# A graph-attention layer with a residual and layer norm: a bound on the scores from sums of squares, W in one transfer, and fewer stores

## The chip, the cores and the metric

The kernel runs on one core of a Trainium2 chip. A core has five engines that run side by side, each through its own list of instructions in order: TensorE (PE, matrix products), VectorE (DVE), ScalarE (ACT), GpSimd (POOL) and SyncE (SP, which here does nothing but issue transfers). Transfers between the large memory (HBM) and the core's own memory run on 16 DMA engines. Matrix products go to a small memory of their own, PSUM. The metric is the device time of one execution in microseconds; lower is better.

## What is computed

`x` is 4096 x 512, `adj` is 4096 x 4096 and stands for a matrix that is added to attention scores, `W` is 512 x 2048 (four heads of 512 columns), `a` is 4 x 1024.

```python
ht = (h @ W).reshape(N, N_HEADS, N_HIDDEN).transpose(1, 0, 2)
src = jnp.einsum('hnd,hd->hn', ht, a[:, :N_HIDDEN, 0])
dst = jnp.einsum('hnd,hd->hn', ht, a[:, N_HIDDEN:, 0])
e = jax.nn.leaky_relu(src[:, :, None] + dst[:, None, :], SLOPE) + adj_mat[None]
att = jax.nn.softmax(e, axis=-1)
h_prime = jnp.einsum('hij,hjd->hid', att, ht)
x = _layernorm(x + h_prime.mean(axis=0), axis=-1)
```

The entries of `adj` are either 0 or random numbers up to 1e9, which is far more than any score from `src` and `dst`. Where the largest entry of a row leads the second by more than the scores can make up, the softmax is exactly 1 at that place and 0 elsewhere. The row's result is then the layer norm of `x` of that row plus (the row of `x` that the largest entry points at) times (the mean of W over the heads).

## The kernel before

The kernel has a fast path, `leading_rows`, and a full one, `general`, which runs only if some row fails the test for a lead (line 66).

*Tiling.* The 4096 rows are 32 blocks of 128, one row a partition. A partition holds the rows 32p to 32p+31, so block `ib` takes the row 32p+ib of each partition, 16 KB of `adj`. The loop (line 432) has 32 steps; step `t` does several stages of different blocks: `segment_maxima` and `find_segment` of block t (VectorE reduces 4096 entries to maxima of segments of 16, 32 or 64, then finds the largest and its segment; GpSimd fetches that segment, `lead`, by an indirect transfer), `find_column` of block t-2 (the place within the segment; GpSimd gathers the row of `x` that it points at, `y`), `turn` and `products` of block t-3 (TensorE transposes `y`, adds `x` as the residual and multiplies by `w_sum`), `stats` of block t-4 and `finish` of two blocks from t-6 (ScalarE: mean, variance, scaling).

*Memory.* One large tile, `hold`, has 32 places of 512 numbers a partition. It first holds W in the places 16 to 31 (`w_at`), then `x` block by block, then the results. `adj` has six buffers (`AHEAD` + 1): the load of block t+6 waits until VectorE is done with block t.

*Order.* The order on each engine is the order in which the code is written (line 55). SP issues almost all transfers into one hardware queue: block 0 of `adj`, half of W, block 1, half of W, blocks 2 to 4, then `x` of blocks 0 to 3 (lines 132 to 143), later one block of `adj` in each step with a few loads of `x` between (line 427). ScalarE issues four loads of `a`, two rows each (line 135). In the built program eight completion semaphores serve the direct transfers of SP and ScalarE in turn, so that a transfer waits for the one that used its semaphore last. Stores are issued after the loop (lines 491 to 496 and 551 to 553).

*The bound.* `mean_of_heads` averages W into `w_sum` at steps 0 to 2. From step 0 to step 14, `turn_a` transposes `a`, and `turn_w` and `head_vector` form, head by head, the product of W's columns with the two halves of `a`: 16 times four transposes, one eviction by ScalarE and eight small products into `pv`. At step 16 `head_norms` takes from these vectors, `v`, the largest sum of norms over the heads, `vn`. After the loop `bound` multiplies `vn` by the largest norm of a row of `x` (`lead_by`), and `test`, `count` and `report` count the rows whose lead is too small. `v` is also handed to `general`.

*The tail.* After the loop come the last blocks: `BEHIND` = 24 and `LATE` = 28; x of blocks 28 to 31 is loaded at step 26, x of 24 to 27 at the last step. The results of blocks 0 to 23 are stored while TensorE and VectorE end blocks 28 to 31; those of 24 to 31 are stored last.

Of the kernel before, what the change touches and what calls it, by code (L numbers as in the profile page):

```python
# [9 lines left out]
F32 = mybir.dt.float32  # L10
# [10 lines left out]
P = 128  # L21
# [8 lines left out]
@with_exitstack  # L30
def gat_resnorm_kernel(
    ctx: ExitStack,
    tc: tile.TileContext,
    x: bass.AP,
    adj: bass.AP,
    W: bass.AP,
    a: bass.AP,
    out: bass.AP,
):

    nc = tc.nc
# [9 lines left out]
    v = keep.tile([P, KB, 2 * H], F32, name="v")  # L59
    n_bad = keep.tile([1, NB], I32, name="n_bad")  # L60
    any_bad = keep.tile([1, 1], I32, name="any_bad")

    leading_rows(tc, x, adj, W, a, out, ident, v, n_bad, any_bad)

    flag = nc.values_load(any_bad[0:1, 0:1], min_val=0, max_val=N)
    with tc.If(flag > 0, preferred_fallthrough_block=True, label="general"):
        general(tc, x, adj, W, out, ident, v, n_bad)


@with_exitstack  # L70
def leading_rows(ctx, tc, x, adj, W, a, out, ident, v, n_bad, any_bad):

# [34 lines left out]
    once.tile([P, 24], F32, name="pad")  # L107
# [5 lines left out]
    once.tile([P, 32], F32, name="pad_end")  # L113
    adj_t = {}

    def pieces(ib):
# [9 lines left out]
    def load_x(lo, n):  # L126
        nc.sync.dma_start(hold[:, ds(lo, n), :], x_rows[:, ds(lo, n), :])

    def load_w(kb, n):
        nc.sync.dma_start(hold[:, ds(w_at + kb * H, n * H), :], w_blocks[:, ds(kb * H, n * H), :])  # L130
# [12 lines left out]
    load_x(0, Q)  # L143

# [192 lines left out]
    def store(queue, lo, n):  # L337
        queue.dma_start(out_rows[:, ds(lo, n), :], hold[:, ds(lo, n), :])
# [7 lines left out]
    at_d = once.tile([P, KB, 2 * H], F32, name="at_d")  # L346
    vn = once.tile([P, 1], F32, name="vn")
    pv = psum.tile([P, KB, 2 * H], F32, name="pv", bufs=1)

    def turn_a():  # L350
        tp = psum.tile([P, KB, P], F32, name="tp", bufs=2)
        for k in range(KB):
            nc.tensor.transpose(tp[:, k, : 2 * H], a_rows[:, ts(k, P)], ident[: 2 * H, : 2 * H])
        nc.scalar.copy(at_d, tp[:, :, : 2 * H])

    def turn_w(kb, h):
        tp = psum.tile([P, KB, P], F32, name="tp", bufs=2)
        for k in range(KB):
# [5 lines left out]
    def head_vector(kb, h, wt):  # L364

        for k in range(KB):
            nc.tensor.matmul(  # L367
                pv[:, kb, h : 2 * H : H], wt[:, k, :], at_d[:, k, h : 2 * H : H],
                start=(k == 0), stop=(k == KB - 1),
            )  # L370

    def head_norms():
        nc.vector.tensor_copy(v, pv)
        vv = once.tile([P, KB, 2 * H], F32, name="vv")
        nc.vector.tensor_mul(vv, v, v)
        pn = psum.tile([P, KB, 2 * H], F32, name="px", bufs=1)
        nc.tensor.matmul(pn, ones, vv, start=True, stop=True)
        n2 = once.tile([P, 2 * H], F32, name="n2")
        nc.vector.tensor_reduce(n2, pn.rearrange("p k c -> p c k"), axis=AX.X, op=OP.add)
        nc.scalar.activation(n2, n2, AF.Sqrt)  # L380
# [47 lines left out]
    vectors = [(kb, h) for kb in range(KB) for h in range(H)]  # L428
    vectors_at = {t: 2 if t < 3 else 1 for t in range(1, 15)}
    COLUMN, PROJECT, STATS, FINISH = 2, 3, 4, 6  # L430

    for t in range(NB):
        if t == NB // 2:
            tc.mark_branch_hint_location("general", engines=HINTED)
        if t in x_at:
            load_x(*x_at[t])
        if t + AHEAD == NB - 1:
            load_x(LATE, Q)
        load_adj(t + AHEAD)
        middle = 1 if t == NB - 1 else 2  # L440
        segment_maxima(t, 0, middle)
        if t >= COLUMN:
            find_column(t - COLUMN)
        segment_maxima(t, middle, PIECES)
        pair = FINISH <= t < BEHIND + FINISH and t % 2 == 0
        if pair:
            rstd(slice(t - FINISH, t - FINISH + 2))
        if t == NB - 1:
            for ib in (BEHIND, BEHIND + 2):
                load_x(ib, 2)  # L450
        find_segment(t)
        if t < 2:
            mean_of_heads(t)
# [100 lines left out]


@with_exitstack
def general(ctx, tc, x, adj, W, out, ident, v, n_bad):

# [6 lines left out]
    nc = tc.nc  # L565
    N, D = x.shape
    KB, NB, NCH, Q = D // P, N // P, N // C, C // P
    H = v.shape[2] // 2
# [5 lines left out]
    w_sb = const.tile([P, KB, H * D], F32, name="w_sb")  # L574
    x_blocks = x.rearrange("(nb p) d -> p nb d", p=P)
    w_blocks = W.rearrange("(kb p) m -> p kb m", p=P)

    with ExitStack() as pre:
        sd_all = pre.enter_context(tc.tile_pool(name="all", bufs=1)).tile([2 * H, N], F32, name="sd_all")
# [3 lines left out]
            nc.gpsimd.dma_start(x_sb[:, ts(g, Q), :], x_blocks[:, ts(g, Q), :])  # L583
        for kb in range(KB):
            nc.gpsimd.dma_start(w_sb[:, kb, :], w_blocks[:, kb, :])
        for g in range(NCH):
            xT = two.tile([P, KB, C], F32, name="xT")
            for q in range(Q):
                ps = pps.tile([P, KB, P], F32, name="ps_x")
                for kb in range(KB):  # L590
                    nc.tensor.transpose(ps[:, kb, :], x_sb[:, g * Q + q, ds(kb, P, KB)], ident)
# [115 lines left out]
```

## Time and profile before

| what | value |
|---|---|
| median of 3 runs | 235.49 us (235.22 to 236.12) |
| the profiled execution | 234.9 us |
| its span, first to last instruction | 233.4 us |
| TensorE busy | 199.9 us (86%) |
| VectorE busy | 191.3 us (82%) |
| ScalarE busy | 111.8 us (48%) |
| GpSimd busy | 100.7 us (43%) |
| moved by DMA | 97.12 MB, mean 416 GB/s |
| of it through SP's queue | 88.08 MB |
| of it through GpSimd's queue | 8.84 MB |

The profile is of one execution. Its span leaves out what lies before the first and after the last instruction of the program, which is why the execution's own time is 1.5 us longer. Busy times are sums over the span, so they don't tell which engine sets the end in a given stretch; the chain of waits and the windows do. An idle engine costs nothing where another sets the pace.

### The profile page before, as it was taken

How to read it: one execution, taken by the hardware profiler on the slowest of the kernel's cores; microseconds unless marked ns; L12 is line 12 of the kernel's file. 1: busy time of each engine (PE TensorE's matmuls, PEld its weight loads, DVE VectorE, ACT ScalarE, POOL GpSimd, SP SyncE). 2: the span in 40 equal slices, each digit the busy share in tenths (PEclk: the TensorE clock that was granted, in tenths of full speed). 3: DMA queues.
4: the chain of work that ended last, by engine and by line, in shares of the span. 5: the costliest groups of instructions: out<-in, count | busy, mean ns of one | idle time of the engine just before them, and what ended most of it. 6: DMA issues, size and time to landing. Idle time of an engine off the chain costs nothing.

```text
span 233.4 us, 2484 instructions
## 1 busy us (share of the span) xinstructions
PE 199.9 (86%) x683; PEld 105.3 (45%) x683; DVE 191.3 (82%) x300; ACT 111.8 (48%) x267; POOL 100.7 (43%) x215
## 2 busy tenths in 40 slices
PE   0069995999999999999999779879998977999980
PEld 0034644646565555665645244334443433444460
DVE  0548299689929999999788995999999999998881
ACT  2001223014474757575767455545664644188561
POOL 2020234414524464644543452647464564548300
PEclk9999999579999999999999979999999999999997
DMA  6999999999999999999999999999999999999995
GB/s 237 423 432 428 428 438 426 415 439 436 422 421 437 423 431 425 431 419 428 430 430 428 432 423 432 423 430 421 426 433 420 426 423 426 412 424 420 421 414 213
DMA packets 12257, 97.12 MB, mean 416 GB/s; under 512 B 1992, under 2 KB 2440, under 8 KB 6480
## 3 DMA queue, kind: packets, MB, share of 16 engines
q1 hardware_dynamic: 8640, 88.08, 89.1%
q0 software_dynamic: 3584, 8.84, 9.6%
q8 instruction: 6, 0.10, 0.2%
q14 instruction: 11, 0.09, 0.1%
q10 hardware_dynamic: 16, 0.02, 0.0%
HBM read 88.54 MB, written 8.39 MB: 415 GB/s over the span
## 4 chain that ended last, share of the span: by engine, by line
DMA 64%; DVE 21%; PE 11%; SPq 1%; issue 1%; ACT 0%; DVEq 0%
DMA adj_t<-in_adj_dram 53%; DVE seg L180 17%; DMA hold<-in_x_dram 11%; PE o L253 6%; PE o L295 2%; DVE at L189 1%; PE tp L238 1%; DVE top L187 1%; PE o L246 1%; DVE within L223 1%; SPq L130 1%; PE o L291 0%; SPq L124 0%; DVE inner L217 0%; ACT hold L335 0%
## 5 line engine op out<-in xcount | busy, mean ns | idle before, releaser
L180 DVE TENSOR_REDUCE seg<-adj_t 128x128 f32<-128x2048 f32 (+3 forms) x66 | 145.5, 2208 | 28.5 <-DMA adj_t<-in_adj_dram 28.2
L253 PE MATMUL o<-w_sum,yt 128*128 128x512 f32 x248 | 117.6, 616 | 0.7 <-ACT yt L240 0.7
L253 PEld LDWEIGHTS o<-w_sum,yt 128*128 128x128 f32 x248 | 45.6, 196 | 55.2 <-issue 43.9
L240 ACT COPY yt<-tp 128x512 f32<-128x512 f32 x32 | 18.8, 588 | 43.9 <-PE tp L238 43.8
L200 POOL DMA_INDIRECT lead<-in_adj_dram,row x32 | 32.3, 1008 | 14.6 <-POOL row L196 14.6
L211 POOL DMA_INDIRECT y<-in_x_dram,col x32 | 30.9, 964 | 15.4 <-POOL col L225 15.1
L238 PE MATMUL tp<-ident,y 128*128 128x128 f32 x128 | 22.1, 296 | 10.2 <-DMA y<-in_x_dram,col 10.1
L246 PE MATMUL o<-hold,ident 128*128 128x512 f32 x52 | 28.5, 634 | 1.7 <-DMA hold<-in_x_dram 1.7
L343 PE MATMUL o<-hold,ident 128*128 128x512 f32 x32 | 17.3, 696 | 13.6 <-DMA hold<-in_L_gnn_W_dram 13.6
L238 PEld LDWEIGHTS tp<-ident,y 128*128 128x128 f32 x128 | 18.5, 209 | 22.8 <-issue 20.5
L361 ACT COPY wt<-tp 128x512 f32<-128x512 f32 x16 | 9.2, 587 | 38.2 <-PE tp L359 38.2
L196 POOL TENSOR_TENSOR row<-at,first 128x1 uint32<-128x1 uint32 x32 | 6.1, 190 | 43.6 <-DVE at L189 43.6
L367 PEld LDWEIGHTS pv<-at_d,wt 128*128 128x128 f32 x128 | 17.2, 200 | 7.4 <-ACT wt L361 3.7
L260 ACT ACTIVATE sq<-hold 128x512 f32<-128x512 f32 x32 | 19.8, 620 | 0.0
L225 POOL TENSOR_TENSOR col<-start,within 128x1 uint32<-128x1 uint32 x31 | 5.9, 190 | 32.2 <-DVE within L223 32.2
L286 ACT ACTIVATE hold<-o,nm,sd 128x512 f32<-128x512 f32 x24 | 17.2, 771 | 0.0
L277 ACT ACTIVATE sq<-o,nm 128x512 f32<-128x512 f32 x24 | 16.5, 687 | 0.8
L343 PEld LDWEIGHTS o<-hold,ident 128*128 128x128 f32 x32 | 6.9, 225 | 21.5 <-issue 21.5
L367 PE MATMUL pv<-at_d,wt 128*128 128x2 f32 x128 | 16.0, 249 | 0.6 <-ACT wt L361 0.6
L344 ACT ACTIVATE w_sum<-o 128x512 f32<-128x512 f32 x4 | 2.4, 598 | 27.5 <-PE o L343 27.5
L275 ACT ACTIVATE sq<-o 128x512 f32<-128x512 f32 x24 | 14.5, 606 | 0.0
L187 DVE MAX8 top<-seg 128x8 f32<-128x256 f32 (+2 forms) x32 | 11.6, 362 | 1.1
(86 smaller groups left out, 140.0 us busy)
## 6 DMA issues: line engine op xcount, KB each, us to landing
adj_t<-in_adj_dram SPq DMA_DIRECT2D x28, 2048.0 KB, 30.8
adj_t<-in_adj_dram SPq DMA_DIRECT2D x6, 1024.0 KB, 28.1
hold<-in_L_gnn_W_dram SPq DMA_DIRECT2D x2, 2048.0 KB, 16.4
hold<-in_x_dram SPq DMA_DIRECT2D x2, 2048.0 KB, 37.6
out_dram<-hold SPq DMA_DIRECT2D x4, 1024.0 KB, 16.1
out_dram<-hold SPq DMA_DIRECT2D x7, 512.0 KB, 14.4
hold<-in_x_dram SPq DMA_DIRECT2D x3, 1024.0 KB
adj_t<-in_adj_dram SPq DMA_DIRECT2D x4, 512.0 KB, 19.8
```

Source lines behind the costliest of these rows:

```text
L180: nc.vector.tensor_reduce(seg_of[ib][:, ts(k, N // e // n)], adj_t[ib][:, ts(k, N // n)].rearrange("p (s e) -> p s e", e=e), axis=AX.X, op ...
L200: nc.gpsimd.indirect_dma_start(out=lead, out_offset=None, in_=adj_segs[e], in_offset=bass.IndirectOffsetOnAxis(ap=row[:, :1], axis=0),)
L211: nc.gpsimd.indirect_dma_start(out=y, out_offset=None, in_=x, in_offset=bass.IndirectOffsetOnAxis(ap=col[:, :1], axis=0),)
L238: nc.tensor.transpose(tp[:, kb, :], y[:, ds(kb, P, KB)], ident)
L240: nc.scalar.copy(yt, tp)
L246: nc.tensor.matmul(o_ps[ib], ident, hold[:, ib, :], start=start, stop=False)
L253: nc.tensor.matmul(o_ps[ib], yt_of[ib][:, kb, :], w_sum[:, kb, :], start=(start and kb == 0), stop=(kb == KB - 1),)
L260: nc.scalar.activation(sq, hold[:, ib, :], AF.Square, accum_out=xx[:, ib : ib + 1])
L277: nc.scalar.activation(sq, o, AF.Square, bias=nm[:, i], accum_out=sd[:, i])
L286: nc.scalar.activation(hold[:, ib, :], o_ps.pop(ib), AF.Identity, bias=nm[:, i], scale=sd[:, i])
L343: nc.tensor.matmul(o, ident, hold[:, w_at + kb * H + h, :], start=(h == 0), stop=(h == H - 1))
L367: nc.tensor.matmul(pv[:, kb, h : 2 * H : H], wt[:, k, :], at_d[:, k, h : 2 * H : H], start=(k == 0), stop=(k == KB - 1),)
```

## The change

Four things are changed.

- The vectors `v` are no longer formed in the fast path. In their place ScalarE squares W and sums the squares (`square_w`, 16 times, in the steps that `turn_w` had) and squares `a` (`square_a`, step 0). `head_norms` takes, for each head, the root of the sum of W's squares times the sum of the roots for the two halves of `a`. By the inequality of Cauchy and Schwarz this is never smaller than the norms used before. `general` forms `v` itself.
- W comes in one transfer of 4 MB, ahead of block 1 of `adj`. `a` is read as eight rows in order, by seven transfers in place of four.
- The results of blocks 8 to 15 are stored by two transfers of four blocks in place of four of two.
- Padding tiles (`pad`, `pad_end`) keep `hold` and the `adj` buffers at the addresses that they had.

```diff
-    for s in range(2):
-        for h in range(0, H, H // 2):
-            nc.scalar.dma_start(
-                a_rows[ds(s * H + h, H // 2), :], a[ds(h, H // 2), ts(s, D), :].rearrange("h d o -> h (d o)")
-            )
-    for kb in range(0, KB, 2):
-        load_w(kb, 2)
-        load_adj(kb // 2 + 1)
-    for ib in range(KB // 2 + 1, AHEAD):
+    for lo in (0, 2):
+        load_a(lo, 2 - lo // 2)
+    nc.sync.dma_start(hold[:, ds(w_at, KB * H), :], w_blocks)
+    load_adj(1)
+    for lo in range(3, 2 * H):
+        load_a(lo, 1)
+    for ib in range(2, AHEAD):
         load_adj(ib)
     load_x(0, Q)
...
-    def turn_w(kb, h):
-        tp = psum.tile([P, KB, P], F32, name="tp", bufs=2)
-        for k in range(KB):
-            nc.tensor.transpose(tp[:, k, :], hold[:, w_at + kb * H + h, ts(k, P)], ident)
-        wt = rows.tile([P, KB, P], F32, name="wt")
-        nc.scalar.copy(wt, tp)
-        return wt
...
+    def square_w(kb, h):
+        sq = rows.tile([P, D], F32, name="sq")
+        nc.scalar.activation(sq, hold[:, w_at + kb * H + h, :], AF.Square, accum_out=w_sq[:, h, kb : kb + 1])
+
+    def square_a():
+        sq = rows.tile([P, D], F32, name="sq")
+        nc.scalar.activation(sq[: 2 * H, :], a_rows, AF.Square, accum_out=a_sq)
 
     def head_norms():
-        nc.vector.tensor_copy(v, pv)
-        vv = once.tile([P, KB, 2 * H], F32, name="vv")
-        nc.vector.tensor_mul(vv, v, v)
...
+        wh = once.tile([P, H], F32, name="wh")
+        nc.vector.tensor_reduce(wh, w_sq, axis=AX.X, op=OP.add)
+        a_diag = once.tile([2 * H, 2 * H], F32, name="a_diag")
+        nc.vector.tensor_scalar(a_diag, ident[: 2 * H, : 2 * H], a_sq, None, op0=OP.mult)
+        pn = psum.tile([P, 3 * H], F32, name="px", bufs=1)
+        nc.tensor.matmul(pn[:, : 2 * H], ones[: 2 * H, :], a_diag, start=True, stop=True)
+        nc.tensor.matmul(pn[:, 2 * H :], ones, wh, start=True, stop=True)
+        n = once.tile([P, 3 * H], F32, name="n")
+        nc.scalar.activation(n, pn, AF.Sqrt)
         both = once.tile([P, H], F32, name="both")
-        nc.vector.tensor_add(both, n2[:, :H], n2[:, H:])
+        nc.vector.tensor_add(both, n[:, 0 : 2 * H : 2], n[:, 1 : 2 * H : 2])
+        nc.vector.tensor_mul(both, both, n[:, 2 * H :])
         nc.vector.tensor_reduce(vn, both, axis=AX.X, op=OP.max)
...
         if t == 0:
-            turn_a()
-        turned = [(*vectors[0], turn_w(*vectors.pop(0))) for _ in range(vectors_at.get(t, 0))]
+            square_a()
+        for _ in range(squares_at.get(t, 0)):
+            square_w(*squares.pop(0))
...
-        for some in turned:
-            head_vector(*some)
...
-    for ib in range(0, 2 * Q, Q):
-        store(nc.sync, ib, Q)
-    for ib in range(2 * Q, 4 * Q, 2):
-        store(nc.sync, ib, 2)
-    for ib in range(4 * Q, BEHIND, Q):
+    for ib in range(0, BEHIND, Q):
         store(nc.sync, ib, Q)
```

`load_a` is new: `nc.scalar.dma_start(a_rows[ds(lo, n), :], a_blocks[ds(lo, n), :])`, with `a_blocks` the eight rows of `a`, head by head.

More of the change, by code (lines that the diff above doesn't have):

```diff
@@ L58, in gat_resnorm_kernel, with leading_rows @@
     ident = keep.tile([P, P], F32, name="ident")
-    v = keep.tile([P, KB, 2 * H], F32, name="v")
     n_bad = keep.tile([1, NB], I32, name="n_bad")
     any_bad = keep.tile([1, 1], I32, name="any_bad")
-    leading_rows(tc, x, adj, W, a, out, ident, v, n_bad, any_bad)
+    leading_rows(tc, x, adj, W, a, out, ident, n_bad, any_bad)
     flag = nc.values_load(any_bad[0:1, 0:1], min_val=0, max_val=N)
     with tc.If(flag > 0, preferred_fallthrough_block=True, label="general"):
-        general(tc, x, adj, W, out, ident, v, n_bad)
+        general(tc, x, adj, W, a, out, ident, n_bad)
 @with_exitstack
-def leading_rows(ctx, tc, x, adj, W, a, out, ident, v, n_bad, any_bad):
+def leading_rows(ctx, tc, x, adj, W, a, out, ident, n_bad, any_bad):
     nc = tc.nc
@@ L104, in leading_rows @@
     w_blocks = W.rearrange("(p kb) (h d) -> p (kb h) d", p=P, h=H)
-    once.tile([P, 24], F32, name="pad")
+    a_blocks = a.rearrange("h (s d) o -> (h s) (d o)", s=2)
+    once.tile([P, 56], F32, name="pad")
     hold = once.tile([P, NB, D], F32, name="hold")
@@ L111, in leading_rows @@
     a_rows = once.tile([2 * H, D], F32, name="a_rows")
-    once.tile([P, 32], F32, name="pad_end")
+    once.tile([P, 48], F32, name="pad_end")
     adj_t = {}
@@ L127, in load_x, with load_a @@
         nc.sync.dma_start(hold[:, ds(lo, n), :], x_rows[:, ds(lo, n), :])
-    def load_w(kb, n):
-        nc.sync.dma_start(hold[:, ds(w_at + kb * H, n * H), :], w_blocks[:, ds(kb * H, n * H), :])
+    def load_a(lo, n):
+        nc.scalar.dma_start(a_rows[ds(lo, n), :], a_blocks[ds(lo, n), :])
     load_adj(0)
-    for s in range(2):
-        for h in range(0, H, H // 2):
-            nc.scalar.dma_start(
-                a_rows[ds(s * H + h, H // 2), :], a[ds(h, H // 2), ts(s, D), :].rearrange("h d o -> h (d o)")
-            )
-    for kb in range(0, KB, 2):
-        load_w(kb, 2)
-        load_adj(kb // 2 + 1)
-    for ib in range(KB // 2 + 1, AHEAD):
+    for lo in (0, 2):
[5 more added lines that the diff above has]
+    for ib in range(2, AHEAD):
         load_adj(ib)
@@ L344, in mean_of_heads @@
         nc.scalar.activation(w_sum[:, kb, :], o, AF.Copy, scale=1.0 / H)
-    at_d = once.tile([P, KB, 2 * H], F32, name="at_d")
     vn = once.tile([P, 1], F32, name="vn")
-    pv = psum.tile([P, KB, 2 * H], F32, name="pv", bufs=1)
-    def turn_a():
-        tp = psum.tile([P, KB, P], F32, name="tp", bufs=2)
-        for k in range(KB):
-            nc.tensor.transpose(tp[:, k, : 2 * H], a_rows[:, ts(k, P)], ident[: 2 * H, : 2 * H])
-        nc.scalar.copy(at_d, tp[:, :, : 2 * H])
-    def turn_w(kb, h):
-        tp = psum.tile([P, KB, P], F32, name="tp", bufs=2)
-        for k in range(KB):
-            nc.tensor.transpose(tp[:, k, :], hold[:, w_at + kb * H + h, ts(k, P)], ident)
-        wt = rows.tile([P, KB, P], F32, name="wt")
-        nc.scalar.copy(wt, tp)
-        return wt
@@ L364, in head_vector @@
[L364 to L370, printed above, removed]
-    def head_norms():
-        nc.vector.tensor_copy(v, pv)
-        vv = once.tile([P, KB, 2 * H], F32, name="vv")
-        nc.vector.tensor_mul(vv, v, v)
[L376 to L380, printed above, removed]
+    w_sq = once.tile([P, H, KB], F32, name="w_sq")
@@ new lines, in leading_rows @@
+    a_sq = once.tile([2 * H, 1], F32, name="a_sq")
+    def square_w(kb, h):
[4 more added lines that the diff above has]
+        nc.scalar.activation(sq[: 2 * H, :], a_rows, AF.Square, accum_out=a_sq)
+    def head_norms():
+        wh = once.tile([P, H], F32, name="wh")
[7 more added lines that the diff above has]
+        nc.scalar.activation(n, pn, AF.Sqrt)
@@ L427, in leading_rows @@
     x_at = {Q - 1: (Q, 2 * Q), 3 * Q - 1: (3 * Q, Q), 4 * Q - 1: (4 * Q, 2 * Q)}
-    vectors = [(kb, h) for kb in range(KB) for h in range(H)]
-    vectors_at = {t: 2 if t < 3 else 1 for t in range(1, 15)}
+    squares = [(kb, h) for kb in range(KB) for h in range(H)]
+    squares_at = {t: 2 if t < 3 else 1 for t in range(1, 15)}
     COLUMN, PROJECT, STATS, FINISH = 2, 3, 4, 6
@@ L556, in general @@
 @with_exitstack
-def general(ctx, tc, x, adj, W, out, ident, v, n_bad):
+def general(ctx, tc, x, adj, W, a, out, ident, n_bad):
     nc = tc.nc
@@ L567, in general @@
     KB, NB, NCH, Q = D // P, N // P, N // C, C // P
-    H = v.shape[2] // 2
+    H = a.shape[0]
     const = ctx.enter_context(tc.tile_pool(name="const", bufs=1))
@@ L576, in general @@
     w_blocks = W.rearrange("(kb p) m -> p kb m", p=P)
+    v = const.tile([P, KB, 2 * H], F32, name="v")
     with ExitStack() as pre:
@@ L585, in general @@
             nc.gpsimd.dma_start(w_sb[:, kb, :], w_blocks[:, kb, :])
+        a_g = two.tile([2 * H, D], F32, name="a_g", bufs=1)
+        for s in range(2):
+            nc.gpsimd.dma_start(a_g[ts(s, H), :], a[:, ts(s, D), :].rearrange("h d o -> h (d o)"))
+        ps = pps.tile([P, KB, P], F32, name="ps_x")
+        for k in range(KB):
+            nc.tensor.transpose(ps[:, k, : 2 * H], a_g[:, ts(k, P)], ident[: 2 * H, : 2 * H])
+        at_d = two.tile([P, KB, 2 * H], F32, name="at_d", bufs=1)
+        nc.scalar.copy(at_d, ps[:, :, : 2 * H])
+        for kb in range(KB):
+            pv = pps.tile([P, Q, 2 * H], F32, name="ps_s")
+            for h in range(H):
+                ps = pps.tile([P, KB, P], F32, name="ps_x")
+                for k in range(KB):
+                    nc.tensor.transpose(ps[:, k, :], w_sb[:, kb, ds(h * D + k * P, P)], ident)
+                wt = two.tile([P, KB, C], F32, name="xT")
+                nc.scalar.copy(wt[:, :, :P], ps)
+                for k in range(KB):
+                    nc.tensor.matmul(
+                        pv[:, 0, h : 2 * H : H], wt[:, k, :P], at_d[:, k, h : 2 * H : H],
+                        start=(k == 0), stop=(k == KB - 1),
+                    )
+            nc.vector.tensor_copy(v[:, kb, :], pv[:, 0, :])
         for g in range(NCH):
@@ L590, in general @@
                 for kb in range(KB):
-                    nc.tensor.transpose(ps[:, kb, :], x_sb[:, g * Q + q, ds(kb, P, KB)], ident)
+                    nc.tensor.transpose(ps[:, kb, :], x_sb[:, g * Q + q, ts(kb, P)], ident)
                 nc.scalar.copy(xT[:, :, ts(q, P)], ps)
```

## The prediction

> **What bounds the kernel now.** I read the page's parts 2 and 3 first, then the chain of waits, then windows at the two ends of the span.
>
> Part 2 and part 3, the DMA rows:
>
> ```profile
> DMA  6999999999999999999999999999999999999995
> GB/s 237 423 432 428 428 438 426 415 439 436 422 421 437 423 431 425 431 419 428 430 430 428 432 423 432 423 430 421 426 433 420 426 423 426 412 424 420 421 414 213
> ...
> q1 hardware_dynamic: 8640, 88.08, 89.1%
> q0 software_dynamic: 3584, 8.84, 9.6%
> ```
>
> Every slice but the first and the last is full at 412 to 439 GB/s. Nothing in the middle of the kernel can end earlier unless bytes go, packets get cheaper, or a slice runs dry. The change moves the same 97.12 MB.
>
> The chain of waits, in order of time:
>
> ```profile
> 3.17 24.89 DMA adj_t<-in_adj_dram
> ...
> 107.84 34.79 DMA adj_t<-in_adj_dram
> ...
> 147.42 28.81 DMA adj_t<-in_adj_dram
> ...
> 176.29 25.22 DMA hold<-in_x_dram
> 201.51 0.04 issue
> 201.55 1.98 PE o L246 x4
> ...
> 223.21 3.55 PE o L295 x16
> ```
>
> Each load lands 25 to 35 us after its issue: five or six blocks are always queued. The last load that TensorE waits for (x of blocks 28 to 31) lands at 201.5, and from there TensorE works without a pause to 226.8. Two clocks therefore end together: the stores in the DMA queue, and this TensorE chain.
>
> Windows, columns PE, PEld, DVE, ACT, POOL busy, PEclk, DMA share, GB/s:
>
> ```profile
> 2.00:4.00 2.00, 0.00 (x0) 0.00 (x0) 0.00 (x0) 1.28 (x1) 0.38 (x6) 1.00 0.86 287
> 4.00:6.00 2.00, 0.00 (x0) 0.00 (x0) 0.00 (x0) 0.00 (x0) 0.00 (x0) 1.00 0.92 393
> 6.00:8.00 2.00, 0.00 (x0) 0.00 (x0) 0.00 (x0) 0.00 (x0) 0.00 (x0) 1.00 1.04 446
> ...
> 228.00:229.00 1.00, 0.00 (x0) 0.00 (x0) 0.61 (x2) 0.56 (x1) 0.00 (x0) 1.00 1.02 412
> 229.00:230.00 1.00, 0.00 (x0) 0.00 (x0) 0.00 (x0) 0.00 (x0) 0.00 (x0) 1.00 0.77 305
> 230.00:231.00 1.00, 0.00 (x0) 0.00 (x0) 0.00 (x0) 0.00 (x0) 0.00 (x0) 0.92 0.73 283
> 231.00:232.00 1.00, 0.00 (x0) 0.00 (x0) 0.00 (x0) 0.00 (x0) 0.00 (x0) 0.50 0.13 49
> ```
>
> All the bandwidth that is missing lies here. At 428 GB/s the stretch 2 to 6 us would have carried 1.71 MB and carried 1.36: 0.8 us. From 229 to 232 about 0.64 MB went, 1.5 us' worth, in the 2.3 us until the data ended: 0.8 us. Recovering everything is worth 1.6 us.
>
> **What the Trainium skill says.** "DMA: Bandwidth & Descriptors", Specifications, gives a fabric ceiling of 435 GB/s; the trace's 428 over 40 to 135 us agrees and leaves 1.6%. The same page, Why small descriptors are slow, tells of a fixed cost per packet; the packet records agree: 2 KB takes 84 ns, 4 KB 159, 8 KB 309, 16 KB 611, so some 8 ns a packet. Queues, rings and completion order says that each DMA engine takes its queues in turn, a packet each; the last gathers below rest on it, and the trace can't confirm it directly. How the engine count k follows from the slowest dimension (Why a DMA increments its semaphore by 16): the loads of `a` show data packets in pairs of 2 KB, which fits two engines for two rows.
>
> **The change part by part.**
>
> *TensorE's work on the head vectors goes.* 4 transposes of `a`, 64 of W (273 ns each), 128 products (L367, 16.0 us busy), 16 evictions (9.2 us) leave steps 0 to 14. TensorE is busy 91.80 of the 95 us from 40 to 135 and shows no wait over 0.3 us between 41 and 135.4, where it has caught up and waits 2.69 us for a gather of y; what it gains earlier it waits away by then. DMA is at 1.01 in that window, and no load waits for it. Worth 0.
>
> *ScalarE squares in its place.* 16 squares of W, one of `a`. The row of the same operation (L260) has 620 ns and a 190 ns read of the accumulator, so 0.71 to 0.81 us each, 12 to 14 us in place of 9.4. ScalarE is busy 50.88 of those 95 us; the 0.2 us more in a step lie in its idle time. x over W's first half is loaded at 102.6 and now also waits for ScalarE's squares, but for the first eight, issued by step 6, some 50 us before. The square of `a` waits for all seven loads of `a`; behind it stand the evictions of `mean_of_heads`, first due near 25 us, and the slowest load of `a` had come by 9 before. Cost 0; without that cover, some 0.2 us a step. `head_norms` keeps five VectorE operations, and TensorE gets one more tiny product: 0.1 us at step 16, hidden.
>
> *W in one transfer.* Before, `adj` of block 1 landed at 18.34, behind half of W. Now all of W is ahead: 2.1 MB or 4.9 us more, so 23.2. Block 1 takes VectorE 5.5 us, to 28.7; block 2 landed at 28.07, so VectorE starts it 0.6 us late. It makes that good at block 5, where it waited 2.67 us for `adj` (47.62). Loads that wait for VectorE start 0.6 us late into a queue of 25 us. `mean_of_heads` starts at 18.3, not 13.6, with all of W there, and ends near 35; its first user comes at 41. Cost 0. Packets: 256 of 16 KB at 611 ns are 9.78 us over 16 engines; 128 of 32 KB at an estimated 1,213 (twice 611 less one overhead) are 9.70. Gain 0.07, or 0 if they are cut at 16 KB.
>
> *Order and semaphores at the start.* In the built programs eight completion semaphores serve all direct transfers in turn, and a transfer first waits for the last user of its own. Before, W's halves and block 1 were issued at once (1.42 to 3.12). Now seven loads of `a` and block 0 take the eight; W waits for the first load of `a`, and block 1 for block 0 (8.67, W then still running). The first load of `a` had landed by 3.17, since block 2, which waited for it, was issued then. So W is issued near 3.2, while block 0 feeds the engines until about 8. Behind W on SP wait all further loads, none of them due before 18. Cost 0; a faster ramp[...] could give up to 0.8, a slower one cost about 0.3. I take 0. The single-row loads of `a` probably spread over 16 engines, 6 small packets and 6 completions on each: 0.1 to 0.2 us of every engine, against 0.37 on two engines before. I take 0.
>
> *Stores of 8 to 15.* 512 packets of 4 KB (159 ns) become 256 of 8 KB (309): 81.4 less 79.1 us over 16 engines, a gain of 0.14. Three transfers fewer with 16 completions of 9 ns are 0.03. They are issued earlier (two by about 204 in place of four until 207), into a full queue: no gain. The last store is issued when ScalarE ends at 228.8 in both; only the queue in front of it shrinks.
>
> *The last gather.* y of block 31, issued at 214.56, landed at 221.49; TensorE was free for it at about 221.7. Its four packets an engine take turns with store packets. With packets of 309 instead of 159 ns it can land up to 4 x 0.15 = 0.6 us later, so up to 0.4 on the TensorE chain; 0 if store traffic there is already the mix of 8 KB (it is, from about 219). I take 0.1.
>
> Sum: -0.07 - 0.14 - 0.03 + 0.1, about -0.15 us, on a profiled execution of 234.9 (span 233.4, 1.5 outside). The median of the runs is 235.49; I keep the difference and say 235.3.
>
> **Rivals.**
>
> *A, both ends of the queue fill (faster).* For it: 0.8 us of missing bandwidth at either end, and fewer transfers queued at the start. Against it: the last store is released by compute. Time: 235.5 - 0.8 (ramp) - 0.2 (packets) - 0.4 (half the end) = 234.1.
>
> *B, W starves the queue (slower).* The first load of `a` moved its data at 2.0, but the other three only at 6.1 to 8.1, behind work of SP. If W's release came as late, at 8.8, its data would start near 10.2 (1 us after issue, plus the issue) with block 0 finished by about 8.1: 2 us dry, nothing later makes it up, 237.5. It decides once W is issued after about 7 us. Against it: the same load, at the same place, had landed by 3.17.
>
> *C, the bound fails.* The new bound is larger: root of W's squares times norm of `a` gives 59.2 where the vectors gave 2.6. With the inputs as the reference draws them the needed lead grows from 179 to 1,674, and the smallest gap of any row is 10,880. No row goes to `general`; were it otherwise the time would be off by far more than a few per cent. Chance below 0.01.
>
> **How the numbers follow.** Forecast (no change, 234.6 to 236.0): 0.7. A: 0.18. B and smaller losses like it (the gather at its full 0.4 with a slower ramp, 236.2): 0.11. C: 0.01. About 0.5%, 1.2 us, is what a measurement here tells from no change. Of the forecast's share nearly all lies within it; A reaches beyond it in most of its cases. Faster 0.18, same 0.71, slower 0.11. The range for 8 in 10 runs from A's 234.1 to 236.3.
>
> **What would show it.** Block 1's first reduction near 23.2 and block 2's near 28.7 in the timeline; the wait before block 5 shorter by 0.6; no slice below 412 between the first and the last; x of 28 to 31 landing at 201 to 201.6; the last store issued at 228.5 to 229.2. TensorE's busy time lower by some 24 us with the span unchanged is the heart of it. I am wrong if W's issue stands after 7 us, if the first windows carry well over 287 and 393 GB/s, or if TensorE pauses before the last transposes.

## The result, and the profile after

| | before | after |
|---|---|---|
| median of the runs, us | 235.22 (22 runs, 234.99 to 236.16) | 235.87 (22 runs, 235.35 to 237.50) |
| ratio after / before, 95% interval | | 1.0027 (1.0016 to 1.0038) |
| span of the profiled execution, us | 233.4 | 234.8 |
| TensorE busy, us | 199.9 | 180.2 |
| traced instructions of TensorE, with its weight loads and semaphores | 1416 | 1025 |

The change made the kernel slower by 0.65 us, 0.27%. The forecast was 235.3 us, 0.15 us faster than the kernel before. The change is within the 0.5% of the likeliest case and within the range, but the interval of the ratio leaves out the forecast: the sum had the wrong sign.

The first parts of the page of the changed kernel, with the row of engines, the DMA rows over the 40 slices, and three queues (packets, MB, share of 16 engines' time):

```profile
PE 180.2 (77%) x489; PEld 82.7 (35%) x489; DVE 190.8 (81%) x300; ACT 114.3 (49%) x284; POOL 100.9 (43%) x215
...
DMA  6999999999999999999999999999999999999984
GB/s 241 470 391 431 408 434 431 424 431 431 424 426 430 428 426 424 435 418 438 422 437 428 419 433 421 433 428 425 433 426 415 426 424 420 419 424 426 423 329 190
...
q1 hardware_dynamic: 8208, 88.08, 88.5%
...
q8 instruction: 5, 0.08, 0.1%
```

The bytes are the same and the packets of q1 fall by 432: 128 for W, 256 for the stores, 48 for the completions of three transfers. So W does go in packets of 32 KB; their median is 1,218 ns, where 1,213 was estimated. The two slices of 470 and 391 belong together, since a large packet is counted where it begins. The middle is as full as before, with one exception, the 408 near 26 us. The new thing is the end: the last slice but one carries 329 GB/s where it carried 414. The last line of the fence counts fetches of instructions; the profile before has 6. The prediction didn't look at it.

The chain of waits of the changed kernel, its last long pieces (start, length, what):

```profile
204.84 5.86 DMA lead<-in_adj_dram,row
...
211.06 2.37 DVE col L229 x2
213.42 6.35 DMA lead<-in_adj_dram,row
...
221.29 0.22 PE px L405 x2
221.51 2.77 PE o L251 x6
...
225.61 3.55 PE o L293 x16
```

Before, this stretch was a TensorE that worked without a pause from 201.5. Now it is the chain of the last two gathers of `lead`, for blocks 30 and 31. The test for a lead on VectorE needs the last one, and TensorE counts the rows that pass it (line 405, `count`) before it goes on with the products of block 30. The waits of VectorE in the changed kernel say the same (total, times, longest):

```profile
DVE within L221 <- DMA lead<-in_adj_dram,row: 2.0, 2, 1.1
DVE inner L215 <- DMA lead<-in_adj_dram,row: 1.6, 2, 1.2
```

VectorE now stands waiting for `lead` of the last blocks; in the kernel before its only such wait is of 0.2 us. TensorE's last products begin at 225.61 and the last store is issued at 231.21, where it was 228.80.

### The profile page after: what moved, and what is told of

Its sections match the earlier page's. It is cut to its first block, busy times and chain, and to the rows that moved or that the text cites. A ratio compares the mean times of both kernels' runs of the same rounds, so it can differ in the third digit from the quotient of the medians.

```text
span 234.8 us, 2105 instructions
## 1 busy us (share of the span) xinstructions
PE 180.2 (77%) x489; PEld 82.7 (35%) x489; DVE 190.8 (81%) x300; ACT 114.3 (49%) x284; POOL 100.9 (43%) x215
## 4 chain that ended last, share of the span: by engine, by line
POOL 32%; issue 31%; DMA 22%; PE 9%; DVE 2%; ACT 2%; ACTq 1%; POOLq 1%; DVEq 0%
DMA hold<-in_x_dram 12%; POOL lead L198 10%; POOL y L209 10%; DMA lead<-in_adj_dram,row 5%; PE o L251 5%; DMA a_rows<-in_L_gnn_a_dram 4%; POOL sd L279 4%; POOL row L194 2%; POOL start L205 2%; POOL col L223 2%; PE o L293 2%; PE o L244 1%; POOL sd L278 1%; DVE col L229 1%; POOL nm L280 1%
## 5 line engine op out<-in xcount | busy, mean ns | idle before, releaser
L236 PE MATMUL tp<-ident,y 128*128 128x128 f32 x128 | 23.1, 305 | 25.7 <-DMA y<-in_x_dram,col 25.7
L209 POOL DMA_INDIRECT y<-in_x_dram,col x32 | 30.9, 964 | 16.7 <-POOL col L223 16.1
L236 PEld LDWEIGHTS tp<-ident,y 128*128 128x128 f32 x128 | 19.1, 209 | 46.2 <-issue 39.6
L244 PE MATMUL o<-hold,ident 128*128 128x512 f32 x52 | 29.2, 650 | 1.6 <-DMA hold<-in_x_dram 1.6
L341 PE MATMUL o<-hold,ident 128*128 128x512 f32 x32 | 16.0, 664 | 18.4 <-DMA hold<-in_L_gnn_W_dram 18.4
L341 PEld LDWEIGHTS o<-hold,ident 128*128 128x128 f32 x32 | 6.8, 216 | 26.8 <-issue 26.8
L273 ACT ACTIVATE sq<-o 128x512 f32<-128x512 f32 x24 | 14.5, 602 | 0.0
L185 DVE MAX8 top<-seg 128x8 f32<-128x256 f32 (+2 forms) x32 | 11.6, 361 | 1.1
L187 DVE FIND_INDEX8 at<-top,seg 128x8 uint32<-128x256 f32 (+2 forms) x32 | 11.3, 353 | 0.4 <-issue 0.4
L279 POOL TENSOR_TENSOR sd<-sd,power 128x2 f32<-128x2 f32 (+1 forms) x13 | 9.6, 737 | 1.1
L244 PEld LDWEIGHTS o<-hold,ident 128*128 128x128 f32 x52 | 9.0, 211 | 2.8 <-ACT sq L350 1.8
```

The costliest lines, as they stand in the source:

```text
L209: nc.gpsimd.indirect_dma_start(out=y, out_offset=None, in_=x, in_offset=bass.IndirectOffsetOnAxis(ap=col[:, :1], axis=0),)
L236: nc.tensor.transpose(tp[:, kb, :], y[:, ds(kb, P, KB)], ident)
L244: nc.tensor.matmul(o_ps[ib], ident, hold[:, ib, :], start=start, stop=False)
L279: nc.gpsimd.tensor_tensor(sd[:, i], sd[:, i], power[:, : i.stop - i.start], op=OP.pow)
```

## The experiments

Each kernel was timed in several rounds beside the kernel before on the same chip; the numbers are ratios to it, with 95% intervals. The chip changed from one group of kernels to the next: one for the four parts below, one for the control and its two companions, one for the four of "The relief, or the banks", and two for the tiny transposes. "One fetch" and "two fetches" below are packets of the queue q8 after 220 us in the profile of that kernel. The theories named in the expectations are these. S: the larger packets of the stores slow the last gathers. L: the loads at the start. Q: the squares on ScalarE. R: the relief of TensorE itself. N: any edit of this finely set order costs something. B: the PSUM banks that moved when `pv` went (not the prediction's rival B). F and T came later and are told where they appear.

### The parts alone

Stores alone, in the kernel before:

```diff
-    for ib in range(2 * Q, 4 * Q, 2):
-        store(nc.sync, ib, 2)
+    for ib in range(2 * Q, 4 * Q, Q):
+        store(nc.sync, ib, Q)
```

> The kernel before with one thing changed: blocks 8 to 15 stored by two transfers of four blocks. Theory S (store packets of 8 KB in place of 4 KB slow the last gathers, on which the tail hangs): 0.4 to 0.8 us slower than before; the gathers of lead of block 31 and y of blocks 30 and 31 take 6.0, 6.6 and 6.9 us from issue to end in place of 4.8, 5.9 and 6.6, and the last store is issued 0.5 us or more after 228.8. Theory L (the start is at fault: W and block 1 in another order): no change, within 0.2 us. Theory Q (the squares on ScalarE): no change.

Measured: 1.0003 (0.9990 to 1.0015). Theory S is right about the gathers: in the profile `lead` of block 31 took 5.72 us from issue to its last packet (before 4.79), y of block 31 7.24 (6.57). The ratio doesn't show the 0.4 to 0.8 us that S foretold, but leaves room for 0.35: the medians are 235.57 and 235.21.

Loads alone: the new lines for W and `a` in the kernel before.

> The kernel before with one thing changed: W in one transfer ahead of block 1, and a by seven loads. Theory L: 0.4 to 0.8 us slower, with VectorE behind by some us somewhere between block 20 and block 30. Theory S and theory Q: within 0.2 us of before, 0.05 to 0.15 faster by the DMA's start, which had 0.06 MB more moved at 5 us in the changed kernel.

Measured: 1.0008 (0.9993 to 1.0023). Theory L falls, or is worth at most 0.2%.

Squares alone: `square_w`, `square_a` and the new `head_norms` in place of the head vectors, with the loads and stores of before.

> The kernel before with one thing changed: the bound from sums of squares. Theory Q (ScalarE later, or GpSimd's gathers at other moments): 0.4 to 0.8 us slower. Theory S and theory L: within 0.2 us of before, TensorE's busy time some 20 us lower.

Measured: 1.0020 (1.0007 to 1.0034), median 235.72, highest 237.33. This part alone is slower.

All but the stores: the changed kernel with the stores of the kernel before.

> The changed kernel with the stores of before (blocks 8 to 15 by four transfers of two). Theory S: the whole loss goes, 235.0 to 235.3 against 235.2 of before; last gathers back at 4.8, 5.9 and 6.6 us. Theory L or Q: stays slower by 0.4 to 0.8 us. If two of the parts share the loss, about half of it stays.

Measured: 1.0042 (1.0027 to 1.0057). The loss stays without the 8 KB stores, so S is not its cause.

### A control, and the two halves of the squares' part

The kernel before under another label, as a control:

> The kernel before, unchanged, as a control. The comparison should give 1.000 with an interval of about 0.1% each way. In its profile: the DMA engines without the stalls of 1 to 2 us on half of them (packets of 16 KB that took 1.2 to 2.1 us in place of 0.61) that the profiles of the changed kernel and of its four parts show, if those belong to the change; with one or two such stalls, if they belong to the chip, and then VectorE's last reductions come 0.4 to 1 us later than in the first profile of before.

Measured: 1.0002 (0.9992 to 1.0013).

Neither vectors nor squares; a constant stands where the norm was:

```diff
     def head_norms():
...
+        nc.vector.memset(vn, 60.0)
```

> Leaves the bound out: neither head vectors nor squares, the norm is a constant 60 set by one instruction; all else, loads and stores too, as before. Theory R (relief of TensorE: without the head vectors it runs ahead in steps 1 to 14, gathers and evictions come at other moments, and that costs): slower than before by 0.15 to 0.3%, as with the squares. Theory Q (the squares on ScalarE themselves): no change against before. Theory N (any edit of the finely set order costs some 0.1 to 0.2%): slower by 0.1 to 0.2%.

Measured: 1.0016 (1.0001 to 1.0030).

The 16 squares of W added to the kernel before, which keeps its vectors; nobody reads the squares:

```diff
+        for k in range(vectors_at.get(t, 0)):
+            square_w(*vectors[k])
```

> The kernel before with the 16 squares of W on ScalarE added to the head vectors, their sums unused. Theory Q: slower than before by 0.15 to 0.4%. Theory R: no change, as TensorE keeps its work. Theory N: slower by 0.1 to 0.2%.

Measured: 0.9996 (0.9983 to 1.0009). Q falls. Adding this work to ScalarE costs nothing, and taking TensorE's work away costs 0.2%. So far this spoke for R.

### The relief, or the banks

The changed kernel with the head vectors formed again, unused:

```diff
+            turn_a()
+        turned = [(*squares[k], turn_w(*squares[k])) for k in range(squares_at.get(t, 0))]
...
+        for some in turned:
+            head_vector(*some)
```

> The changed kernel, in which TensorE and ScalarE form the head vectors as before, in the same steps, beside the squares; nobody uses them. TensorE has its 24 us of work back, and PSUM's banks lie as in the kernel before. Theory R (the relief of TensorE costs 0.2 to 0.3%): the loss goes, 1.000 to 1.001 of the kernel before. Theory B (PSUM's banks): the same, since the banks are back. Theory N (any edit of the finely set order costs 0.1 to 0.2%, and they add up): 1.003 or more, since there is one more edit and more work.

Measured: 1.0055 (1.0036 to 1.0074), from six runs. R and B had foretold 1.000 to 1.001, N 1.003 or more. The profile's chain of waits, in order of time:

```profile
54.58 3.54 PE o L251 x8
60.69 3.54 PE o L251 x8
66.80 3.54 PE o L251 x8
```

The groups of products are 6.1 us apart, and so on to 115.8, while VectorE needs 5.7 us for a block (in the profile before, from 55.72, the second half of block 6, to 61.38, that of block 7). So TensorE, which starts at 18.3 when all of W is there, is behind in this stretch. But that doesn't explain the loss: the same 6.1 us stand in the chains of the loads alone (groups at 84.92, 91.03 and 97.13) and of the added squares (54.42, 60.52 and 66.63), which form the vectors too and take 1.0008 and 0.9996. Where this kernel loses its time stays open. It has one fetch in its tail, so the fetches told below don't explain it either, and as another loss covers it, this run can't say what the relief costs.

One line in the changed kernel keeps a PSUM tile where `pv` was, unused, so that all other tiles keep their banks:

```diff
+    psum.tile([P, KB, 2 * H], F32, name="pv", bufs=1)
```

> The changed kernel with one line more: the PSUM tile of the head vectors is still set aside, though nothing is written to it, so that the results, the transposes and the norms lie in the same PSUM banks as in the kernel before. TensorE keeps its relief. Theory B (the banks had moved): 1.000 to 1.001. Theory R: 1.003, as the changed kernel. This tells R from B, which every run so far has mixed.

Measured: 1.0025 (1.0008 to 1.0041). The same line in the kernel with the squares alone:

> The kernel before with the bound from squares alone (which took 1.002), and the unused PSUM tile of the head vectors set aside. Theory B: 1.000. Theory R: 1.002 again.

Measured: 1.0025 (1.0013 to 1.0037). B falls twice. And the changed kernel once more, beside these:

> The changed kernel itself, on the chip of the three others, so that they can be compared with it directly: 1.003 by its first measurement, 235.9 us. Its profile: the stall of half of the DMA engines that was seen in nearly every profile comes again at some time before 90 us, if it belongs to the chip, and not at the 25.9 us of the first profile of this kernel if its place is by chance.

Measured: 1.0014 (0.9995 to 1.0033), median 235.89. The stall came at 33 us in place of 25.9, so its place isn't fixed by the kernel.

### The fetches of instructions

With S, L, Q and B gone, and R's own test blurred, I compared what the kernels on either side have in common. The single runs gave the first hint: the slow kernels are wide. The middle half of the runs of the changed kernel spans 0.70 us (235.69 to 236.39), that of the kernel before beside it 0.33 (235.09 to 235.42).

The second was the line q8. It counts fetches of instructions, 16 KB each, 0.9 to 1.8 us on one DMA engine. They follow TensorE's progress: in the kernel before one comes for every 260 of its traced instructions on average (1041 between the first and the fifth; over all profiles the gaps are 147 to 374, and not every instruction is traced), and one more when it nears the end of its list. The others are called regular here. That they are TensorE's is inferred from this, and from the runs below. Taking the head vectors away takes 391 traced instructions out of TensorE's list, and so moves every later fetch. The DMA view of 220 to 234 us, first of the kernel before:

```profile
q8 instruction: 1, 0.02, 0.5%
```

and of the changed kernel:

```profile
q8 instruction: 2, 0.03, 1.0%
```

In the packet records they lie at 225.9 us before, and at 224.9 and 229.6 after. The last regular fetch of the kernel before is the one at 200.9. All seven profiles taken so far without the vectors (six kernels, one of them twice) had two fetches after 220 us, and all six with vectors (five kernels) had one. Theory F: a regular fetch that falls into the last 12 us costs. It can be tested by tiny transposes on TensorE, which add instructions and little work. In the kernel before, whose place `pv` is free from step 16:

```diff
+        few = pv.rearrange("p k c -> p (k c)")
...
+        if 16 <= t < 26:
+            for _ in range(6):
+                nc.tensor.transpose(few[:8, :8], ident[:8, :8], ident[:8, :8])
```

> The kernel before, with 60 transposes of 8 by 8 more on TensorE, six in each step from 16 to 25, into a PSUM place that is free by then. Theory F (a regular fetch of TensorE's instructions that falls into the last 12 us costs): the traced instructions of TensorE grow by 120, the last regular fetch moves from about 201 us to 222 to 228, there are two such fetches after 220 us in place of one, and the time is 1.001 to 1.003 with a wider spread. Theory R (relief of TensorE costs): no change, 1.000. Theory N (any edit costs): 1.001 to 1.002, but with one fetch after 220 us just as well as with two.

Measured: 1.0016 (0.9994 to 1.0038), median 235.29, one run at 238.3. The fetches lie at 189.7, 224.2 and 227.3 us, as foretold; the time was left open, as the interval holds both 1.000 and 1.003.

The kernel with the squares alone and seven such transposes in each of the ten steps (into the bank kept as above):

> The kernel before with the bound from squares alone (1.002 in its own run), with 70 tiny transposes more, seven in each step from 16 to 25. Theory F: the last regular fetch moves out of the tail, to about 200 to 210 us, one is left after 220 us, and the time comes back to 1.000 with the narrow spread of the kernel before. Theories R and N: 1.002 to 1.003 again, since TensorE has its relief and the edits have grown by one.

Measured: 1.0001 (0.9992 to 1.0009), middle half 235.08 to 235.28. The changed kernel with the same:

> The changed kernel with the same 70 tiny transposes. Theory F: 1.0005 to 1.0015, what the stores and the loads cost by themselves is left. Theories R and N: 1.0025 or more.

Measured: 1.0000 (0.9991 to 1.0008), median 235.08, middle half 235.06 to 235.15. The changed kernel with the stores of before, with the same:

> The changed kernel with the stores of the kernel before (1.0042 in its own run), with the same 70 tiny transposes. Theory F: 1.000 to 1.001, as the loads alone. Theories R and N: 1.003 to 1.005.

Measured: 1.0014 (1.0005 to 1.0022), where it was 1.0042. The loss shrinks but doesn't go: F had said at most 1.001. In these three kernels the last regular fetch lies at 201 us. The tiny transposes in the profile of the changed kernel that has 70 of them (shortest, median and longest in ns, first and last start in us):

```profile
L466 PE MATMUL pv<-ident x70: 164/165/171, 125.7 to 179.3; 8*8 8x8 f32 x70
```

and q8 in its DMA view of 220 to 234 us:

```profile
q8 instruction: 1, 0.02, 0.7%
```

They are not free: 70 times 165 ns are 11.6 us of TensorE. So theory T stood against F: they help because they keep TensorE busier. More of them tell the two apart, if so many that a regular fetch comes into the tail again. The changed kernel with 125, five in each step from 1 to 25:

```diff
-        if 16 <= t < 26:
-            for _ in range(7):
+        if 1 <= t < 26:
+            for _ in range(5):
```

> The changed kernel with 125 tiny transposes in place of 70, five in each step from 1 to 25. TensorE's traced instructions grow to 1275, so one more regular fetch comes near the 1241st, at 222 to 227 us, with the one at the end after it: two after 220 us, as in the changed kernel. Theory F: slow and wide again, 1.002 to 1.003. Theory T (the transposes help because they keep TensorE busier): 1.000, as with 70.

Measured: 1.0030 (1.0015 to 1.0046), middle half 235.38 to 236.11. Its DMA view of 220 to 234 us:

```profile
q8 instruction: 2, 0.03, 1.1%
```

The squares alone with 125:

> The kernel before with the bound from squares alone and the same 125 tiny transposes in place of 70. Theory F: two fetches after 220 us and 1.002 again, where 70 gave 1.0001. Theory T: 1.000.

Measured: 1.0020 (1.0008 to 1.0033), with two fetches. And the kernel before with its 60 once more:

> The same kernel as in the run of the kernel before with 60 tiny transposes (1.0016, interval 0.9994 to 1.0038), again. Theory F: 1.001 to 1.003, two fetches after 220 us. Else: 1.000.

Measured: 1.0019 (1.0007 to 1.0031), with two fetches. T as foretold falls, since more transposes brought the loss back; they also stand in other steps, five a step in place of seven, so that a T of the late steps alone isn't excluded by these two. N falls too, as one edit more made the changed kernel as fast as the kernel before. F gave the place of the fetches each time, and the direction of the time wherever the interval can tell; the size it missed twice, with 1.0000 where it said 1.0005 to 1.0015 and 1.0014 where it said at most 1.001:

| kernel | traced TensorE instructions | last regular fetch: before which, at what us | fetches after 220 us | ratio |
|---|---|---|---|---|
| before | 1416 | 1237, 200.9 | 1 | 1 |
| after | 1025 | 984, 224.9 | 2 | 1.0027 |
| after, 70 tiny | 1165 | 985, 201.1 | 1 | 1.0000 |
| after, 125 tiny | 1275 | 1241, 224.6 | 2 | 1.0030 |
| all but the stores | 1025 | 989, 224.3 | 2 | 1.0042 |
| all but the stores, 70 tiny | 1165 | 985, 200.7 | 1 | 1.0014 |
| squares alone | 1025 | 1010, 226.6 | 2 | 1.0020 |
| squares alone, 70 tiny | 1165 | 985, 200.9 | 1 | 1.0001 |
| squares alone, 125 tiny | 1275 | 1241, 224.5 | 2 | 1.0020 |
| before, 60 tiny, again | 1536 | 1496, 226.2 | 2 | 1.0019 |

It is not the number of fetches: the changed kernel has five with 70 tiny transposes and five without; the kernel before has six, and so has the changed kernel with 125. It is not TensorE's busy time (184.2 us with 70, 186.5 with 125). It is not the granted clock: the means of the slow kernels of this table are 0.94 to 0.97, of the others with tiny transposes 0.94 to 0.96. What the slow kernels share is that TensorE's list ends shortly after a regular fetch. Few lengths were tried: lists of 1017 to 1025, 1275 and 1536 traced instructions lost time, lists of 1165 and of 1416 or 1417 lost little or none (but for the one of 1421 that has vectors and squares both), and nothing between was measured.

One rival stands untested. All kernels with 60 or 70 tiny transposes were timed on one chip, those with 125 and the repetition with 60 on another, and neither the squares alone nor, so far as is known, the changed kernel was timed on either. On the first chip the kernel with two fetches (1.0016) isn't told from those with one (1.0000 to 1.0014). The kernel with 60 tiny transposes lay 0.12 us above the kernel before there (medians), and 0.42 us on the second. So part of what 70 seem to mend may be the chip, and on the second chip N would fit the three numbers as well as F. The 70 and the 125 side by side on one chip would settle it.

That the late fetch itself takes the time isn't shown, and the profiles speak against the plain form of it. The changed kernel around its regular fetch at 224.9 us, in its DMA view of 224 to 225.5 us:

```profile
q1 hardware_dynamic: 84, 0.50, 80.2%
q8 instruction: 1, 0.02, 5.4%
q14 instruction: 1, 0.01, 1.4%
```

No packet of a gather (q0) is left beside it: y of block 31 had ended at 223.2. In ten of the eleven profiles with two fetches the last gather's data had ended and the last transposes had begun before the regular fetch in the tail began. From the last transposes to the last store's issue all profiles take 7.1 to 7.2 us, with one fetch and with two. From the last store's issue to the end they take 3.9 us on average with two and 4.0 with one (without the kernel that has vectors and squares both). The mean span is 0.4 us longer with two (234.2 against 233.8), and that difference lies before the last transposes. In the changed kernel, for example, `lead` of block 31 was issued 4.33 us after VectorE's end of block 31 (before 3.58), while no fetch of TensorE was under way. So the place of the fetch goes with the loss, and how it would cost time is open; a profile is one execution out of runs that differ by more than 1 us. No version was found that beats the kernel before by more than the measurement tells.

## Why the prediction was wrong

*"TensorE's work on the head vectors goes. Worth 0."* This is the step that failed. As engine time it is right: in the changed kernel TensorE waits 25.7 us for y in all, before 10.1, and nothing ends earlier. But taking the work out made the kernel slower: 1.0016 with nothing in its place and 1.0020 with the squares, while on the same two chips the edits that keep the vectors took 0.9996 to 1.0008. On a third chip the squares took 1.0025, with the bank kept. The term was 0 and measured about +0.4 to +0.6 us. The step counted only what the instructions do, not that they are instructions. Without them TensorE's last regular fetch moved from 200.9 to 224.9 us, and with tiny transposes that moved it back the changed kernel took 1.0000 in place of 1.0027. That the loss follows the length of TensorE's list is what the runs show best, with the reserve about the chips; why it does stays open.

*The rest of the sum, about -0.15 us.* With the fetch out of the tail the changed kernel takes 1.0000 (0.9991 to 1.0008). The forecast of 0.9994 lies within. Three kernels with 70 tiny transposes, timed side by side, split it: squares alone 235.17 us in the median, with the new loads 235.50, with the new loads and stores 235.08. So there the loads cost about 0.3 us, where the sum said -0.07, and the stores gave 0.4, where it said 0.17 less 0.1 for the last gather. That the sum came out near is then the luck of two errors of opposite sign. In the kernel before the stores alone gave no gain (1.0003).

*ScalarE's squares, cost 0.* Right for the 16 squares of W: 0.9996 when they are added alone.

*W in one transfer.* Right in its times: W is issued at 3.03 us (said: near 3.2), and the timeline of VectorE in the changed kernel shows blocks 1 and 2 where they were worked out, 23.2 and 28.7 (start, length, then the idle time before in brackets):

```profile
23.20 4.48 DVE L178 TENSOR_REDUCE seg<-adj_t 128x128 f32<-128x2048 f32 x2 [9.25 <-DMA adj_t<-in_adj_dram]
...
28.59 2.27 DVE L178 TENSOR_REDUCE seg<-adj_t 128x128 f32<-128x2048 f32 x1
```

The wait before block 5 was 1.64 us, where it was 2.67. TensorE's later start costs little even with all its old work: the loads alone take 1.0008 (0.9993 to 1.0023). The guess that the single rows of `a` spread over 16 engines was wrong: each row went as one packet of 2 KB with one completion, and the last was done at 16.7 us (in the kernel before by 9), still ahead of the evictions due near 25.

*The last gather, "up to 0.4; I take 0.1".* Too small as a delay, and the wrong gather. The step looked at y of block 31 alone. Before it stands `lead` of block 31, slowed in the same way: 4.79 to 5.98 us, y from 6.57 to 6.91. And it is `lead`, through the test and the count at 221.29, that TensorE waits for; y of block 31 had landed before TensorE was free for it. From VectorE's end of block 31 to the last transposes it took 13.2 to 13.6 us in the six profiles with the old stores and one fetch, and 14.1 and 14.5 in the two with the new stores and one fetch (without the kernel that has vectors and squares both). The page of the Trainium skill that the prediction named for this, "DMA: Bandwidth & Descriptors", section Queues, rings and completion order, says that an engine serves its queues in turn, a packet each; slower gathers beside larger packets fit that, though no run shows the turns themselves. What it costs in time isn't clear: the stores alone take 1.0003, with medians 0.36 us apart. In the kernel before the last store's data waited for the queue (from its issue to the end 4.56 us); in the changed kernel and with the stores alone, whose chain is late, it takes 3.58 and 3.37 us.

*Signs named in advance.* Against the prediction came a slice of 408 GB/s near 26 us, one of 329 at the end, the last store at 231.21 (said: at most 229.2), and TensorE's pauses before the last transposes (0.84 us at 219.20 for y, 0.51 for the count). The first is a stall of DMA engines told below, which the control shows too; the others are the late chain of gathers. The first windows also carried more, 297 and 435 GB/s where it was 287 and 393; by 6 us that is 0.06 MB by the packet records, 0.14 us' worth. TensorE's busy time fell by 19.7 us (said: some 24). x of blocks 28 to 31 came as foretold: its last packet ends at 201.1, and TensorE, held by a gather at 198.3, used it only at 202.4.

*Rivals.* A didn't come: the start filled by 0.14 us, and the last slices are emptier. (The end of the kernel before lacked more than the 0.8 us of the sum: its last data packet ends at 231.8, not 2.3 us after 229.) B didn't come: W was issued at 3.03. C didn't come. The slower side had 0.11, with the right sign and none of the right reasons.

## What to carry to other kernels

Instructions are data too: they come through the same DMA engines, here 16 KB for about every 260 traced instructions of TensorE, and adding or taking away instructions of TensorE moves its later fetches. When a change that should be free costs some tenths of a per cent and widens the spread, look where the instruction queue's packets fall in the last microseconds, and move them by a few dozen tiny instructions as a test, with all versions on one chip. Then look in the profile for what the fetch holds up: that two things come together doesn't show that one makes the other. Compare parts by undoing them both ways: a part that costs when it is removed and costs nothing when its replacement is added is a sign that what counts is neither part's work.

## What the runs showed of the hardware

- About half of the DMA engines stall together in most profiles: mostly 7 or 8 packets of 16 KB (up to 16), which take 611 ns elsewhere, take 0.9 to 2.1 us at the same moment (up to 2.9 in one profile), at 31 to 34 us (25.9 in the first profile of the changed kernel, 29.6 in one other). Spread over all 16 engines it costs 0.2 to 0.9 us. The control has it; the profile of the kernel before and those of four kernels with tiny transposes don't, the kernel with the new loads and squares among them. So it doesn't come from the change. Those four were taken on one chip, so it may belong to the chip or to the execution.
- A gather's time depends on the packets beside it. `lead` of the last block, 128 rows of 256 bytes in 16 packets of 2 KB, took 4.8 to 5.0 us beside 4 KB stores (5.4 in one profile) and 5.5 to 6.1 beside 8 KB stores.
- A transpose of 8 by 8 takes TensorE 165 ns, against 273 for one of 128 by 128 (medians; the transposes of W in the kernel before).
